# A second state of a Mamba sum kept in a tile of its own, and another queue and pace for the convolution weights, in a four-layer conv/attention kernel

## The chip, the core and the metric

The kernel runs on one core of a Trainium2 chip. The metric is the device time of one execution in microseconds (us). The core has five engines that run side by side and meet at semaphores: TensorE (PE, with its weight loads shown apart as PEld), VectorE (DVE), ScalarE (ACT), GpSimd (POOL) and SyncE (SP), which here only issues DMA transfers. ScalarE can issue transfers too.

## What is computed

Four layers follow each other on an input x of 2 images, 256 channels, 32 x 32 pixels, all in float32: a vision Mamba block pair (layer 0), a convolution that makes a 7 x 7 attention over neighbours (layer 1), a linear attention with a mixture of experts (layer 2), and a softmax attention with a mixture of experts (layer 3). The change lies in layer 0 and in a preparation for layer 1 that is done meanwhile. Of the reference this is what matters:

```python
# layer 0, twice (m1, m2); u has 1024 tokens an image, 512 inner channels d, 16 states n
xs    = silu(causal_conv4(u @ in_w_left))
dt, Bm, Cm = split(xs @ xproj_w)
delta = softplus(dt @ dt_w + dt_b)
dA    = exp(delta[..., None] * A);  dBu = delta[..., None] * Bm * xs[..., None]
h_t   = dA_t * h_(t-1) + dBu_t                 # for each d and n
y_t   = sum over n of h_t[d, n] * C_t[n]       # einsum('bdn,bn->bd')
out   = ((y + xs * D) * silu(u @ in_w_right)) @ out_w + out_b
# layer 1: a dilated 7x7 convolution (w1) followed by a 1x1 convolution (w2) with 49 outputs
```

The two convolutions of layer 1 have nothing between them, so the kernel first multiplies the weights: w1 and w2 give one 7 x 7 convolution with 49 outputs, the "taps".

## The kernel before, in words

**Units.** The 2048 tokens are cut into four chunks of 512, and each of the two Mamba blocks goes over them, which makes eight units, 0 to 7 (line 608). Inside a unit, `scan` (L415) walks over the 16 states n and, for each, over four groups dc of 128 inner channels: 64 slots. For one state:

- GpSimd makes dBu as two tiles `h` of 128 x 1024 each: du times a broadcast row `b` of B (L461). The rows `b` come from DRAM through SyncE's queue (L457).
- ScalarE makes `da` = exp(delta * A) into PSUM, one 128 x 512 tile a slot (L468).
- VectorE runs the recurrence over the 512 tokens, in place on `h` (L472, one scan a slot).
- TensorE turns `h` so that tokens lie on partitions (L440, 16 transposes a state into four PSUM tiles `ht`).
- The turned tile times C_n is summed into `ya` by VectorE (L449, a multiply-add of 128 x 512, four a state). For two states it is done by ScalarE instead (L447, a copy with a scale): state 0 starts `ya`, and state ASIDE = 10 goes into a tile `yb` of its own, so that VectorE has nothing to do for it. The turning and summing of state n run in the four slots of state n + 1, as the generator `rest` (L434).

There are six buffers of `h`, three of `da`, three of `ht`.

**What is woven in.** While a unit scans, `paced` (L552) hands out steps of other generators by slot: the `back` (L485) of the unit before, the `front` (L293) of the unit after, and the taps. The back's first nine steps (GATED) fall in slots 0 to 35, its other seven in slots 40 to 61; the front's first 22 steps (HEAD) in slots 0 to 38, its last 16 in slots 38 to 62. The front's last steps make delta and du for the next unit: 16 tensor operations on GpSimd (L405, L407, L409, L411) fed by ScalarE (L393, L396, L403, L404). The back multiplies the gate, and for each dc it gathers y on TensorE: one matmul with the diagonal of D (L507), then for `ya` and again for `yb` four matmuls with the identity, that turn the sum back and add it in PSUM (L512). VectorE multiplies the result with the gate (L516). Then come the output matmuls (L524, L528), a norm, and the addition to x on GpSimd (L543, and L548 in block m2, which adds the input x loaded by L547).

**The taps** (`Taps.make`, L675). The weights are 7 x 14 blocks of 128 x 128. A part of four blocks (the last of a row has two) is loaded through SyncE's queue (L686), turned on TensorE (L700), copied by ScalarE (L702), multiplied with w2 (L706), copied by ScalarE (L711) and stored to DRAM through SyncE's queue (L714). That makes 28 parts of two steps each and one last step for the bias. Unit 0 takes 12 steps and units 1 to 6 take 9 each, in slots 40 to 63 (L630, L631). In unit 7 the taps' place is taken by the convolution itself, on TensorE (L650, L762), which reads them back.

The Tile framework orders each engine's instructions by a priority that follows the order of emission and by when it expects a buffer, so an engine's order is near the emitted one but not the same.

Of the kernel before, what the change touches and what calls it, by code (L numbers as in the profile page):

```python
# [19 lines left out]
P = 128  # L20
# [213 lines left out]
class Mamba:  # L234

    ASIDE = 10
    GATED = 9
    HEAD = 22  # L240

# [173 lines left out]
    def scan(self, j, before, between, start=False):  # L415
# [6 lines left out]
        xs, bd, ct, delta, du = self.chunks[j]  # L422
        state, first = self.state, self.first(j)
        ya = self.two.tile([P, TPC, DI], F32, tag="ya", name=f"{m}_ya_{j}")
        yb = self.one.tile([P, TPC, DI], F32, tag="yb", name=f"{m}_yb_{j}")
        self.chunks[j] = xs, ya, yb
        G = 2
        half = [P, G, TC]

# [4 lines left out]
        def rest(n, hs):  # L434


            for i in range(TPC):
                ps = self.ps_ht.tile([P, DI], F32, tag="ht", name=f"{m}_ht_{j}_{n}_{i}")
                for dc in range(NDC):
                    nc.tensor.transpose(  # L440
                        ps[:, dc * P : (dc + 1) * P], hs[dc // G][:, dc % G, i * P : (i + 1) * P],
                        net.ident,
                    )
                yield
                c = ct[:, i, n : n + 1]
                if n in (0, self.ASIDE):
                    nc.scalar.activation((yb if n else ya)[:, i, :], ps, AF.Copy, scale=c)  # L447
                else:
                    nc.vector.scalar_tensor_tensor(  # L449
                        ya[:, i, :], ps, c, ya[:, i, :], ALU.mult, ALU.add  # L450
                    )
                if i == 0 and first:
                    keep(n, hs)

        for n in range(NS):
            b = scanp.tile([P, TC], F32, tag="b", name=f"{m}_b_{j}_{n}", bufs=4)
            nc.sync.dma_start(b, bd[n].partition_broadcast(P))  # L457
            hs = []
            for g in range(NDC // G):
                h = scanp.tile(half, F32, tag="h", name=f"{m}_h_{j}_{n}_{g}", bufs=6)  # L460
                (nc.vector if start and n == 0 else nc.gpsimd).tensor_mul(  # L461
                    h, du[:, g * G : (g + 1) * G, :], b.unsqueeze(1).to_broadcast(half)
                )
                hs.append(h)
            for dc in range(NDC):
                da = self.ps_da.tile([P, TC], F32, tag="da", name=f"{m}_da_{j}_{n}_{dc}")
                i = dc * NS + n
                nc.scalar.activation(  # L468
                    da, delta[:, dc, :], AF.Exp, scale=self.aneg[:, i : i + 1]
                )  # L470
                h = hs[dc // G][:, dc % G, :]
                nc.vector.tensor_tensor_scan(  # L472
                    h, da, h, 0.0 if first else state[:, n, dc : dc + 1], ALU.mult, ALU.add
                )
# [10 lines left out]
    def back(self, j):  # L485
# [19 lines left out]
        for dc in range(NDC):  # L505
# [4 lines left out]
            for k, ya in enumerate(sums):  # L510
                for i in range(TPC):
                    nc.tensor.matmul(  # L512
                        ps[:, i * P : (i + 1) * P], lhsT=ya[:, i, dc * P : (dc + 1) * P],
                        rhs=net.ident, start=False, stop=(k == 1 and i == TPC - 1),
                    )
            nc.vector.tensor_mul(y[:, dc, :], ps, gate[:, dc, :])  # L516
            yield
# [18 lines left out]
        yield  # L536
        for cc in range(NCC):
            ps = net.transposed(self.ps_mm, tiles, cc, "mm")
            r = self.one.tile([P, TC], F32, tag="r", name=f"{m}_r_{j}_{cc}", bufs=3)
            nc.scalar.activation(  # L540
                r, ps, AF.Identity, scale=net.col(f"{m}_ln_w", cc), bias=net.col(f"{m}_ln_b", cc)
            )
            nc.gpsimd.tensor_add(xt[:, cc, tok], xt[:, cc, tok], r)  # L543
            if self.x is not None:
                x = self.one.tile([P, TC], F32, tag="r", name=f"{m}_x_{j}_{cc}", bufs=3)
                at = j % (HW // TC) * TC
                nc.sync.dma_start(x, self.x[j // (HW // TC), cc, :, at : at + TC])  # L547
                nc.gpsimd.tensor_add(xt[:, cc, tok], xt[:, cc, tok], x)  # L548
# [26 lines left out]
def layer0(net, x, x_dram, m1, m2, load_image, taps, conv_dram, lg):  # L575
# [5 lines left out]
    with (  # L581
# [32 lines left out]
        for u, (m, j) in enumerate(units):  # L614
# [12 lines left out]
            steps += [(f, 16, 38, 62) for f in fronts] + [(b, 7, 40, 61) for b in done]  # L627
            steps += [(rest, 1, 62, 63)]
            if u + 1 < len(units):
                n = 9 if u else 12  # L630
                steps += [(islice(aside, n), n, 40, 63)]  # L631
            else:
                last.close()
                m.ps_da = last.enter_context(tc.tile_pool(name="m_da2", bufs=2, space=PSUM))
# [28 lines left out]
class Taps:  # L663
# [11 lines left out]
    def make(self, psum, dram):  # L675

        net, nc, pool = self.net, self.net.nc, self.pool
        self.made = [dram.tile([P, 14, NTAP], F32, name=f"taps_{u}") for u in range(7)]
        parts = [(u, k) for u in range(7) for k in range(0, 14, 4)]
        loaded = []  # L680

        def load():
            u, k = parts[len(loaded)]
            n = min(4, 14 - k)
            w = pool.tile([P, 4, P], F32, tag="w1", name=f"w1_{u}_{k}", bufs=3)
            nc.sync.dma_start(  # L686
                w[:, :n, :], self.w1[:, u, k // NCC : (k + n) // NCC].rearrange("p v c o -> p (v c) o")
            )
            loaded.append(w)

# [2 lines left out]
        for i, (u, k) in enumerate(parts):  # L693
            if len(loaded) < len(parts):
                load()
            w = loaded[i]
            n = min(4, 14 - k)
# [1045 lines left out]
```

## Time and profile before

The time before is 2189.04 us, the median of 3 runs (2184.31 to 2190.55). The profiled execution took 2186.6 us.

| | |
|---|---|
| layer 0 | from the start to about 1110 us |
| eight units, from the first scan to the next unit's first | 112.1, 127.0, 126.4, 124.5, 121.1, 124.8, 124.6, and 117.6 us for the last one's scans |
| granted TensorE clock, mean | 0.918 of full speed |

In the profile each engine's busy time is a union of its instructions. A group of instructions is a line of the kernel on one engine; behind the first bar stand the busy time in us and the mean ns of one instruction, behind the second the idle time of the engine just before them and what ended it. A multiply in float32 appears as two matmul passes, so the 128 identity matmuls of `ya` are counted as 256. On VectorE and ScalarE an instruction starts a little before the one ahead of it ends, so the distance of starts is shorter than the duration.

### The profile page before, as it was taken

Reading aid. Unit: us, or ns where it says so; the run is one execution under the profiler, and the core shown is the slowest. Engines: PE = TensorE matmul, PEld = TensorE weight load, DVE = VectorE, ACT = ScalarE, POOL = GpSimd, SP = SyncE. Lnnn points to the kernel's source line nnn. Section 1 sums busy time; section 2 is a strip of 40 time slices with the busy share of each in tenths; the row PEclk is TensorE's granted clock in tenths of the full one; section 3 lists DMA queues with packets and bytes.
Section 4 is the critical chain, followed back from the end, with each engine's and each line's share of the span. In section 5 each row is a group of like instructions: output and inputs, shape, how many; then the busy total and the mean of one; then the engine's idle time right before and its main releaser. Section 6 shows DMA issues by size and latency. Waiting matters only on the chain.

```text
span 2186.6 us, 27311 instructions
## 1 busy us (share of the span) xinstructions
PE 1894.0 (87%) x9652; PEld 1335.5 (61%) x9652; DVE 1400.3 (64%) x2210; ACT 959.2 (44%) x1610; POOL 1028.9 (47%) x726
## 2 busy tenths in 40 slices
PE   6888898898978888788999989949999599859996
PEld 2464555556555655454646556539999467649995
DVE  6999998999999999899005475752222544432223
ACT  4676677767777767645013454411111132301111
POOL 3796787959698686965025420012332000023331
PEclk9869889898989889899999999969999799979997
DMA  2121121111212111310030100028998200059997
GB/s 106 45 68 39 37 69 35 58 35 45 62 47 60 38 49 35 85 42 17 0 64 1 48 15 10 20 82 306 326 329 323 82 10 10 20 206 327 329 323 292
DMA packets 90499, 223.87 MB, mean 102 GB/s; under 512 B 35467, under 2 KB 51728, under 8 KB 79732
## 3 DMA queue, kind: packets, MB, share of 16 engines
q1 hardware_dynamic: 77636, 198.29, 27.1%
q0 software_dynamic: 7728, 19.15, 2.9%
q10 hardware_dynamic: 4992, 4.59, 0.7%
q8 instruction: 81, 1.33, 0.3%
q14 instruction: 62, 0.51, 0.1%
HBM read 204.60 MB, written 19.37 MB: 102 GB/s over the span
## 4 chain that ended last, share of the span: by engine, by line
PE 32%; DVE 22%; issue 19%; POOL 11%; ACT 10%; DMA 5%; POOLq 0%; SPq 0%; DVEq 0%; ACTq 0%
DVE m_h L472 11%; DVE m_ya L449 6%; PE acc L762 3%; POOL x L1520 3%; POOL l_yd L1570 3%; PE m_ht L440 3%; PE early_acc L762 3%; PE av L1276 3%; ACT m_da L468 2%; PE sc L1250 2%; DMA l_yd<-y,target 2%; POOL m_h L461 2%; PE h L1099 2%; PE m_xd_ps L351 1%; PE w L1108 1%
## 5 line engine op out<-in xcount | busy, mean ns | idle before, releaser
L461 POOL TENSOR_TENSOR m_h<-m_du,m_b 128x1024 f32<-128x1024 f32 x254 | 594.5, 2364 | 196.0 <-PE m_ht L440 95.8
L440 PE MATMUL m_ht<-ident,m_h 128*128 128x128 f32 x2048 | 361.2, 305 | 119.4 <-DVE m_ya L449 83.9
L440 PEld LDWEIGHTS m_ht<-ident,m_h 128*128 128x128 f32 x2048 | 259.5, 154 | 317.8 <-DVE m_ya L449 112.7
L468 ACT ACTIVATE m_da<-m_delta,m_aneg 128x512 f32<-128x512 f32 x512 | 349.5, 690 | 220.8 <-DVE m_h L472 220.1
L1520 POOL DMA_INDIRECT x<-l_zd,source x82 | 84.8, 1034 | 573.1 <-DVE source L1465 217.1
L449 DVE SCALAR_TENSOR_TENSOR m_ya<-m_ht,m_ct,m_ya 128x512 f32<-128x512 f32 x448 | 320.2, 733 | 18.4 <-PE m_ht L440 17.5
L472 DVE TENSOR_TENSOR_SCAN m_h<-m_da,m_state,m_h 128x512 f32<-128x512 f32 x256 | 318.7, 1271 | 14.7 <-POOL m_h L461 8.7
L472 DVE TENSOR_TENSOR_SCAN m_h<-m_da,m_h 128x512 f32<-128x512 f32 x256 | 303.3, 1210 | 23.6 <-ACT m_da L468 13.1
L1550 PEld LDWEIGHTS h<-xts,we 128*128 128x128 f32 x2528 | 298.4, 194 | 7.1 <-issue 3.4
L1550 PE MATMUL h<-xts,we 128*128 128x128 f32 x2528 | 299.4, 277 | 2.2 <-issue 1.7
L1557 DVE TENSOR_TENSOR hid<-hid,h 128x512 f32<-128x512 f32 x79 | 54.3, 688 | 258.9 <-PE h L1550 258.9
L1556 ACT ACTIVATE hid<-h 128x512 f32<-128x512 f32 x79 | 47.2, 598 | 384.6 <-issue 324.0
L1564 PE MATMUL o<-we,hid 128*128 128x256 f32 x632 | 150.4, 380 | 2.2 <-DVE y L1569 1.6
L1570 POOL DMA_INDIRECT l_yd<-y,target x79 | 79.3, 1003 | 142.6 <-DVE y L1569 136.3
L1564 PEld LDWEIGHTS o<-we,hid 128*128 128x128 f32 x632 | 113.7, 190 | 15.7 <-DVE y L1569 2.8
L336 PE MATMUL m_conv<-m_pre,m_taps 128*128 128x512 f32 x240 | 114.6, 596 | 6.7 <-ACT m_gate L498 5.6
L762 PE MATMUL early_acc<-x,early 128*98 128x448 f32 (+21 forms) x308 | 97.0, 447 | 0.0
L762 PE MATMUL acc<-x,pair 128*98 128x416 f32 (+21 forms) x308 | 93.6, 452 | 0.0
L1569 DVE COPY y<-o 128x256 f32<-128x256 f32 x79 | 33.6, 425 | 69.6 <-PE o L1564 69.6
L309 PE MATMUL m_in<-x,m_in_sb 128*128 128x512 f32 x128 | 68.8, 663 | 9.8 <-ACT m_pre L313 6.9
L762 PEld LDWEIGHTS acc<-x,pair 128*98 128x98 f32 x308 | 47.7, 167 | 39.9 <-issue 34.5
L528 PE MATMUL m_out<-m_out_sb,m_xs 128*128 128x256 f32 x256 | 68.7, 397 | 0.0
(318 smaller groups left out, 2843.3 us busy)
## 6 DMA issues: line engine op xcount, KB each, us to landing
we<-in_l_experts_dram SPq DMA_DIRECT2D x82, 1536.0 KB
m_b<-m_bd SPq DMA_DIRECT2D x128, 256.0 KB
w<-in_l_w_dram SPq DMA_DIRECT2D x21, 256.0 KB
l_zd<-l_z SPq DMA_DIRECT2D x7, 512.0 KB
l_yl<-l_yd SPq DMA_DIRECT2D x10, 256.0 KB
l_yl<-l_yd ACTq DMA_DIRECT2D x10, 256.0 KB
early<-taps SPq DMA_DIRECT2D x7, 343.0 KB
pair<-taps SPq DMA_DIRECT2D x7, 343.0 KB
```

The source lines that it names most:

```text
L309: nc.tensor.matmul(ps, lhsT=self.in_sb[:, kc, mc * P : (mc + 1) * P], rhs=self.xt[:, kc, tok], start=(kc == 0), stop=(kc == NCC - 1),)
L336: nc.tensor.matmul(ps, lhsT=self.taps[:, dc * 4 + k, :], rhs=pre[:, dc, k : k + TC], start=(k == 0), stop=(k == 3),)
L440: nc.tensor.transpose(ps[:, dc * P : (dc + 1) * P], hs[dc // G][:, dc % G, i * P : (i + 1) * P], net.ident,)
L449: nc.vector.scalar_tensor_tensor(ya[:, i, :], ps, c, ya[:, i, :], ALU.mult, ALU.add)
L461: (nc.vector if start and n == 0 else nc.gpsimd).tensor_mul(h, du[:, g * G : (g + 1) * G, :], b.unsqueeze(1).to_broadcast(half))
L468: nc.scalar.activation(da, delta[:, dc, :], AF.Exp, scale=self.aneg[:, i : i + 1])
L472: nc.vector.tensor_tensor_scan(h, da, h, 0.0 if first else state[:, n, dc : dc + 1], ALU.mult, ALU.add)
L762: nc.tensor.matmul(a[:, lo - 16 * k : hi - 16 * k, co : co + n], lhsT=lhsT, rhs=self.x[:, kc, b, lo - r0 : hi - r0, ci : ci + n], start=(u ...
L1520: nc.gpsimd.indirect_dma_start(out=x, out_offset=None, in_=zd[:, :], in_offset=bass.IndirectOffsetOnAxis(ap=source[:, g : g + 1], axis=0), ...
L1550: nc.tensor.matmul(ps[:, at], lhsT=w12[:, s, kc, at], rhs=xt[:, kc * P : (kc + 1) * P], start=(kc == 0), stop=(kc == NCC - 1),)
L1564: nc.tensor.matmul(ps[:, :C], lhsT=ht[:, mc * P : (mc + 1) * P], rhs=w[:, 8 + mc, :], start=(mc == 0), stop=(mc == NHC - 1),)
L1570: nc.gpsimd.indirect_dma_start(out=yd[g], out_offset=bass.IndirectOffsetOnAxis(ap=target[:, g : g + 1], axis=0), in_=y, in_offset=None, bo ...
```

## The change

A second state, 13, gets a tile of its own; the other one moves from state 10 to state 9. ScalarE fills both, and the back of each unit adds three sums on TensorE instead of two. The new tile takes 8 KB a partition; to make room, the rows `b` have three buffers instead of four, the tag `r` of the back two instead of three, and the parts of the taps have three blocks instead of four. That makes 35 parts of two steps. Units 1 to 6 take 10 steps each, and all steps are spread over slots 24 to 63 instead of 40 to 63. The made taps are stored through ScalarE's queue. The aim is to take work from VectorE and to keep the taps' stores from standing in SyncE's queue in front of the rows `b`.

```diff
-    ASIDE = 10
+    ASIDE = 9, 13
...
-        yb = self.one.tile([P, TPC, DI], F32, tag="yb", name=f"{m}_yb_{j}")
-        self.chunks[j] = xs, ya, yb
+        sums = {0: ya}
+        for n in self.ASIDE:
+            sums[n] = self.one.tile([P, TPC, DI], F32, tag=f"ya{n}", name=f"{m}_ya{n}_{j}")
+        self.chunks[j] = xs, *sums.values()
...
-                if n in (0, self.ASIDE):
-                    nc.scalar.activation((yb if n else ya)[:, i, :], ps, AF.Copy, scale=c)
+                if n in sums:
+                    nc.scalar.activation(sums[n][:, i, :], ps, AF.Copy, scale=c)
...
-            b = scanp.tile([P, TC], F32, tag="b", name=f"{m}_b_{j}_{n}", bufs=4)
+            b = scanp.tile([P, TC], F32, tag="b", name=f"{m}_b_{j}_{n}", bufs=3)
...
-                        rhs=net.ident, start=False, stop=(k == 1 and i == TPC - 1),
+                        rhs=net.ident, start=False, stop=(k == len(sums) - 1 and i == TPC - 1),
...
-            r = self.one.tile([P, TC], F32, tag="r", name=f"{m}_r_{j}_{cc}", bufs=3)
+            r = self.one.tile([P, TC], F32, tag="r", name=f"{m}_r_{j}_{cc}", bufs=2)
...
-                x = self.one.tile([P, TC], F32, tag="r", name=f"{m}_x_{j}_{cc}", bufs=3)
+                x = self.one.tile([P, TC], F32, tag="r", name=f"{m}_x_{j}_{cc}", bufs=2)
...
-                n = 9 if u else 12
-                steps += [(islice(aside, n), n, 40, 63)]
+                n = 10 if u else 12
+                steps += [(islice(aside, n), n, 24, 63)]
...
-        parts = [(u, k) for u in range(7) for k in range(0, 14, 4)]
+        parts = [(u, k) for u in range(7) for k in range(0, 14, 3)]
...
-            n = min(4, 14 - k)
-            w = pool.tile([P, 4, P], F32, tag="w1", name=f"w1_{u}_{k}", bufs=3)
+            n = min(3, 14 - k)
+            w = pool.tile([P, 3, P], F32, tag="w1", name=f"w1_{u}_{k}", bufs=3)
...
-            wt = pool.tile([P, TC], F32, tag="w1t", name=f"w1ts_{u}_{k}", bufs=1)
+            wt = pool.tile([P, 3 * P], F32, tag="w1t", name=f"w1ts_{u}_{k}", bufs=1)
...
-            out = pool.tile([P, 4, NTAP], F32, tag="taps", name=f"taps_sb_{u}_{k}", bufs=3)
+            out = pool.tile([P, 3, NTAP], F32, tag="taps", name=f"taps_sb_{u}_{k}", bufs=3)
...
-            nc.sync.dma_start(self.made[u][:, k : k + n, :], out[:, :n, :])
+            nc.scalar.dma_start(self.made[u][:, k : k + n, :], out[:, :n, :])
```

More of the change, by code (lines that the diff above doesn't have):

```diff
@@ L683, in load @@
             u, k = parts[len(loaded)]
-            n = min(4, 14 - k)
-            w = pool.tile([P, 4, P], F32, tag="w1", name=f"w1_{u}_{k}", bufs=3)
+            n = min(3, 14 - k)
+            w = pool.tile([P, 3, P], F32, tag="w1", name=f"w1_{u}_{k}", bufs=3)
             nc.sync.dma_start(
-                w[:, :n, :], self.w1[:, u, k // NCC : (k + n) // NCC].rearrange("p v c o -> p (v c) o")
+                w[:, :n, :], self.w1[:, u].rearrange("p v c o -> p (v c) o")[:, k : k + n]
             )
@@ L696, in make @@
             w = loaded[i]
-            n = min(4, 14 - k)
+            n = min(3, 14 - k)
             ps = psum.tile([P, TC], F32, tag="mm", name=f"w1t_{u}_{k}")
```

## The prediction

> **What bounds the kernel now.** I began with the page: the busy shares and the groups of the scan.
>
> ```profile
> PE 1894.0 (87%) x9652; PEld 1335.5 (61%) x9652; DVE 1400.3 (64%) x2210; ACT 959.2 (44%) x1610; POOL 1028.9 (47%) x726
> ...
> L461 POOL TENSOR_TENSOR m_h<-m_du,m_b 128x1024 f32<-128x1024 f32 x254 | 594.5, 2364 | 196.0 <-PE m_ht L440 95.8
> L449 DVE SCALAR_TENSOR_TENSOR m_ya<-m_ht,m_ct,m_ya 128x512 f32<-128x512 f32 x448 | 320.2, 733 | 18.4 <-PE m_ht L440 17.5
> L472 DVE TENSOR_TENSOR_SCAN m_h<-m_da,m_state,m_h 128x512 f32<-128x512 f32 x256 | 318.7, 1271 | 14.7 <-POOL m_h L461 8.7
> ```
>
> Taken alone this says VectorE: its scans and multiply-adds hardly ever wait. But GpSimd waits 95.8 us for turned tiles, so I looked at when it does. The timeline of GpSimd in unit 4 shows it: after a wait of 2.75 us for a free buffer, from the product for state 10 on, it never stops until the next unit has begun.
>
> ```profile
> 613.73 11.66 POOL L461 TENSOR_TENSOR m_h<-m_du,m_b 128x1024 f32<-128x1024 f32 x5 [2.75 <-ACT m_delta L389]
> 625.33 1.30 POOL L405 TENSOR_TENSOR m_du<-m_e,m_du 128x512 f32<-128x512 f32 x1
> ...
> 661.98 4.68 POOL L461 TENSOR_TENSOR m_h<-m_du,m_b 128x1024 f32<-128x1024 f32 x2
> ```
>
> The next unit's first scan starts at 664.37, just when the first of the last two products ends. So each unit has two stretches: A, from its first scan to the product for state 10; B, from there to the next unit's first scan. Busy time by stretches, A and B of units 4 and 5, then unit 7 and the tail behind its last scan (columns: window, length, then busy us and count of PE, PEld, DVE, ACT, POOL, then granted clock, DMA share, GB/s):
>
> ```profile
> 543.20:613.70 70.50, 64.64 (x297) 37.44 (x296) 68.59 (x77) 51.56 (x92) 48.97 (x25) 1.00 0.19 56
> 613.70:664.40 50.70, 40.01 (x220) 30.54 (x219) 46.23 (x61) 40.83 (x73) 50.02 (x31) 0.83 0.17 53
> 664.40:738.30 73.90, 67.41 (x288) 39.02 (x288) 70.55 (x75) 49.54 (x71) 46.77 (x22) 0.93 0.19 47
> 738.30:789.10 50.80, 40.65 (x215) 31.34 (x214) 47.06 (x59) 39.38 (x60) 50.16 (x31) 0.80 0.14 38
> 913.80:1031.30 117.50, 101.38 (x500) 60.64 (x498) 115.19 (x134) 61.10 (x89) 81.96 (x39) 0.99 0.16 40
> 1031.30:1110.20 78.90, 78.80 (x337) 47.46 (x337) 11.49 (x38) 9.74 (x13) 7.38 (x13) 1.00 0.05 13
> ```
>
> B lasts 50.7 or 50.8 us in both, and GpSimd is busy for all but 0.7 of it. That is its work: 13 products of 2.33 (states 10 to 15, and the next unit's first) and 16 operations of about 1.25 for the next unit's delta and du make 50.3. VectorE has 3.7 to 4.5 us to spare in B. In A VectorE (97%) and TensorE (92%) are both nearly full. Unit 7 has no front and is VectorE's (98%); the tail is TensorE's (99.9%).
>
> The chain of work that ended last shows where in A TensorE takes over. These are a step of y in unit 4, the second such in unit 5, and one in the tail:
>
> ```profile
> 590.23 1.92 PE m_xd_ps L351 x4
> 592.14 0.26 PE m_ht L440
> 592.40 0.86 PE m_y L507 x2
> 593.26 1.78 PE m_y L512 x16
> 595.05 0.44 PE m_ht L440 x4
> 595.49 1.85 PE m_xd_ps L351 x4
> ...
> 732.04 2.92 PE m_y L512 x16
> ...
> 1052.36 1.78 PE m_y L512 x16
> ```
>
> TensorE's queue is in order, so the y sums stand in front of the matmuls of x_dbl and of transposes that free `h` for GpSimd. Of four y steps, unit 4 has one on the chain (593), unit 5 two (715.65, and 732.04, which ran in a stretch of half clock).
>
> **What the Trainium skill says.** "TensorE: Matmul & The Clock Gate", Part 1 (engine queue depths): ScalarE, VectorE and GpSimd are strict first-in-first-out, and only weight loads go ahead on TensorE. The trace agrees: GpSimd waits 81.5 us in units 1 to 6 for transposes that stand behind other matmuls. The same part: TensorE's clock drops to half after an idle window. The trace has 1.00 in A of unit 4, 0.93 in A of unit 5 and about 0.8 in B, where TensorE has least to do. "ScalarE: Activation LUTs", What ACT_TABLE_LOAD costs: an activation with one pointer operand is 280 ns plus 0.833 ns an element (707 ns for 512), and successive ones overlap by some 93 ns. The copies of L447 take 0.68, and start 0.57 to 0.62 apart. "DMA: Bandwidth & Descriptors", Issuing engines are not separate DMA queues: another issuer saves only the time of the issue. Here one is 0.40 us on SyncE (L714) and 0.31 on ScalarE (L359).
>
> **The change, part by part.**
>
> - VectorE loses four multiply-adds a unit (states 9 and 13 leave, 10 comes back). In VectorE's timeline their starts are 0.65 us apart: 2.6 us a unit. In units 0 to 6 both states' sums fall in slots 40 to 43 and 56 to 59, which is B, where GpSimd sets the end. A scan can start earlier only as far as its product is ready; at the ends of units 1 to 6 the first product of state 15 is there 0 to 0.5 us before its scan. So I count 0.5 us for each of seven units: -3.5. In unit 7 the whole counts: -2.6.
> - ScalarE gets four more copies (0.6 each, 2.4 a unit). Those of state 9 fall on slots 40 to 43, where it is full (exp and ln of the front, two table loads: busy 8.36 of 8.42 us in unit 4) and VectorE waits 1.2 us for `da`. Queued behind them are `da` for the next scans and L403/L404, which GpSimd's L405 needs. L404 ends at 621.7 and L405 starts at 625.33: 3.6 us of slack, against 2.4 for the copies. The later `da` is hidden too: at states 11 and 12 a product is ready 4 to 7 us before its scan. Nothing.
> - TensorE gets a third sum: per step of y eight more passes. Sixteen take 1.78 us, so 0.89, or 1.46 at half clock. In A, on the chain: one step in even units (0.89), two in odd ones (0.89 + 1.46). Three units of each: 2.7 + 7.0 = +9.7. In unit 7's scans one step on the chain, +0.9. In the tail all four steps are on the chain: 4 x 0.89 = +3.6.
> - The taps leave slots 40 to 63 for 24 to 63: steps are 3.9 slots apart, so four of ten (two parts) are now in A, where none was. A part of three is three transposes (0.60 for four, so 0.45) and six passes (0.84 for eight, so 0.63): 2.2 us a unit on TensorE, and on ScalarE two copies (0.45, 0.25) and an issue (0.31), 2.0 a unit. If all lay on the chain, 2.2 a unit or +13; if TensorE's idle time in A (5.9 and 6.5 us) took it, nothing. I take a third: +4. What the end of the units gains (VectorE's waits for `da` behind bunched taps) lies in B behind GpSimd: nothing.
> - The store on ScalarE adds 35 issues of 0.31 us and waits for its own copy; behind it is `da`, mostly ahead of the scan by 0.5 to 3 us. What it frees on SyncE's queue held up nobody: no wait for `b` shows, and in units 1 to 6 a row is issued 16 us or more ahead of its product. Three buffers make that about two products, 9 us in a row at the least, and x of 256 KB landed 3.76 us after its issue. Nothing. With two `r` buffers the second x is loaded only once the first is added. GpSimd has an addition and a product (3.5 us) in between: at most 0.5 us, in two units. Nothing.
>
> Sum: -3.5 - 2.6 + 9.7 + 0.9 + 3.6 + 4 = +12, so 2201 us.
>
> **The rivals.** *VectorE is the bound.* Its 98% in unit 7 and its small idle time speak for it; then 2.6 us is saved in all eight units, -20.8, the tail gives back 3.6, and 2172 comes out. Against it: B is the same 50.7 us in units with different VectorE work. *TensorE's idle time in A takes the sums and the taps.* 5.9 us is there and 3.6 + 2.2 is asked for; left are -3.5 - 2.6 + 0.9 + 3.6, about 2187, no change. Against it: TensorE's idle time is waiting for others, not to be filled at will. *ScalarE delays GpSimd.* If the four copies, a taps copy and an issue all get in front of L404 (2.4 + 0.8 + 0.3) and the `da` queue, L405 waits and B grows 1 to 2 us in units 0 to 6; with the main case's terms that is about 2211.
>
> **How the numbers follow.** Main case 0.45; VectorE bound 0.28; idle time 0.17; ScalarE 0.10. Faster by over 0.3% (below 2182.5): the VectorE case and a little of the next, since extra TensorE work can also keep the clock up in A of odd units: 0.31. Within: 0.18. Slower (above 2195.6): 0.51, the main case less its lower part, and ScalarE's. The range goes from just under the VectorE case, 2170, to all the taps on the chain and some delay by ScalarE, 2216.
>
> **What would show it.** B should stay at 50 to 51 us with GpSimd full, though VectorE's busy time there falls by about 2.6; A should grow, odd units more; the chain should have L512 x24 with 2.7 us a step; the tail should grow by 3.6. I am wrong if B gets shorter (GpSimd's order changed, or it wasn't the bound), if A shrinks (clock, or the taps' new place), or if GpSimd shows waits for ScalarE in B.

## The result and the profile after

The changed kernel takes 2250.97 us, the median of 4 runs (2249.59 to 2252.14); the kernel before, run beside it, takes 2189.6 (2184.31 to 2190.55). The ratio is 1.0285, with a 95% interval of 1.0267 to 1.0303: slower by 62 us. Forecast were 2201, at most 2216. The direction was right, the size was off by 50 us.

All of the loss lies in layer 0. From the trace of each kernel, in us (A and B as in the prediction; the last column is everything behind the tail):

| | A, units 1 to 6 | B, units 1 to 4 | B, units 5 and 6 | unit 0 | scans of unit 7 | tail | rest |
|---|---|---|---|---|---|---|---|
| before | 442.1 | 204.3 | 102.0 | 112.1 | 117.6 | 78.9 | 1076.4 |
| after | 465.2 | 211.9 | 127.7 | 114.0 | 117.1 | 84.0 | 1074.9 |
| difference | +23.1 | +7.6 | +25.7 | +1.9 | -0.5 | +5.1 | -1.5 |

The page of the changed kernel, busy shares and the groups of the scan, to lay beside those of before:

```profile
PE 1927.2 (86%) x9908; PEld 1361.9 (61%) x9908; DVE 1383.0 (62%) x2178; ACT 981.8 (44%) x1656; POOL 1028.6 (46%) x726
...
L463 POOL TENSOR_TENSOR m_h<-m_du,m_b 128x1024 f32<-128x1024 f32 x254 | 594.6, 2365 | 244.1 <-PE m_ht L442 114.5
...
L474 DVE TENSOR_TENSOR_SCAN m_h<-m_da,m_state,m_h 128x512 f32<-128x512 f32 x256 | 317.0, 1266 | 34.8 <-ACT m_da L470 23.6
...
L451 DVE SCALAR_TENSOR_TENSOR m_ya<-m_ht,m_ct,m_ya 128x512 f32<-128x512 f32 x416 | 295.8, 731 | 36.5 <-PE m_ht L442 36.0
```

GpSimd works as much as before (1028.6 against 1028.9) and waits longer. VectorE has its 32 multiply-adds less, 17 us of work, but the idle time before its scans that start from a kept state (the second row) and before its multiply-adds has about doubled (14.7 to 34.8, 18.4 to 36.5). So no single instruction runs slower; the engines wait more for each other.

The stretches show where: A and B of units 4 and 5, and the tail (columns as in the prediction).

```profile
561.50:637.20 75.70, 68.71 (x329) 42.07 (x329) 68.56 (x77) 51.80 (x93) 46.59 (x24) 0.95 0.17 51
637.20:689.90 52.70, 39.53 (x206) 26.85 (x204) 43.60 (x56) 42.00 (x74) 50.60 (x31) 0.90 0.19 53
689.90:767.00 77.10, 69.13 (x330) 42.19 (x330) 70.82 (x77) 50.83 (x75) 46.27 (x22) 0.96 0.16 43
767.00:829.10 62.10, 44.21 (x204) 31.70 (x203) 44.73 (x55) 41.60 (x64) 56.29 (x35) 0.75 0.19 55
...
1088.90:1172.90 84.00, 83.97 (x371) 51.41 (x370) 10.66 (x36) 11.13 (x15) 7.39 (x13) 1.00 0.04 12
```

B of unit 4 has grown by 2.0 us, and GpSimd, which filled it before, now has 2.1 us idle in it. B of unit 5 has grown by 11.3. A of unit 4 has grown by 5.2 and A of unit 5 by 3.2.

The plainest account is VectorE's waits from the first scan of unit 0 to the last of unit 7. Before, and then after:

```profile
DVE m_h L472 <- POOL m_h L461: 19.2, 13, 4.9
DVE m_h L472 <- ACT m_da L468: 19.0, 23, 2.5
DVE m_ya L449 <- PE m_ht L440: 17.5, 26, 2.2
```

```profile
DVE m_h L474 <- ACT m_da L470: 47.2, 22, 10.2
DVE m_ya L451 <- PE m_ht L442: 36.0, 34, 3.3
DVE m_h L474 <- POOL m_h L463: 23.9, 16, 3.6
DVE ln_st L160 <- PE m_out L530: 21.8, 6, 5.3
```

(Columns: us in total, times, longest.) The units last 978.0 us before and 1035.8 after, +57.8. VectorE is busy for 919.4 and 902.9, so 16.5 less: the saving is real. Its idle time goes from 58.6 to 132.9, +74.3, and the rows say for what: ScalarE's `da` +28, turned tiles from TensorE +19, the output matmuls (for the norm's statistics, L160) +22, GpSimd's products +5. The new waits take 4.5 times what the work gave. Of the 47.2 us for `da`, 18.6 are two waits that come from the buffers of `r` (below); without them `da` has grown by 9.6 only.

**What the output matmuls' row hides.** Here is ScalarE in unit 4 of the changed kernel, at state 10:

```profile
639.65 1.91 ACT L393 ACTIVATE m_e<-m_e 128x2048 f32<-128x2048 f32 x1
...
643.04 2.01 ACT L396 ACTIVATE m_ln<-m_e,one 128x2048 f32<-128x2048 f32 x1
...
645.57 0.67 ACT L449 ACTIVATE m_ya<-m_ht,m_ct 128x512 f32<-128x512 f32 x1
...
646.75 0.46 ACT L704 COPY w1ts<-w1t 128x384 f32<-128x384 f32 x1
...
647.82 1.28 ACT L470 ACT_TABLE_LOAD   x1
649.12 0.69 ACT L470 ACTIVATE m_da<-m_delta,m_aneg 128x512 f32<-128x512 f32 x1
```

and VectorE at the same time:

```profile
649.36 0.43 DVE L160 BATCH_NORM_STATS2 ln_st<-m_out 128x6 f32<-128x256 f32 x1 [3.66 <-PE m_out L530]
649.84 1.22 DVE L474 TENSOR_TENSOR_SCAN m_h<-m_da,m_h 128x512 f32<-128x512 f32 x1
```

Two copies of state 9 (at 645.57 and 647.11) and one of the taps stand between the front's `ln` and the table load behind which `da` waits, so the first `da` runs from 649.12 to 649.81. In VectorE's queue a statistic of the norm stands ahead of the next scan; the matmuls it needs end at 649.3 on TensorE, which is busy 10.3 of the 11.8 us of this state. So the row gives the 3.66 us to the output matmuls, but the scan starts at 649.84, 0.03 us after its `da`: without the statistic it would have waited as long. In the six places where this wait shows, five scans start 0.02 to 0.04 us after their `da` has ended; only in unit 6 was `da` ready before. In these five ScalarE is what was waited for, and the wait for the output matmuls lies in its shadow. The state takes 11.75 us where it took 8.42; over units 1 to 6 it takes 12.1 where it took 8.4, 22 us in all.

The copies of state 9 explain less than half of this. The same instructions of ScalarE before, where the state begins at 616.48 (after: 639.62):

```profile
615.12 1.91 ACT L393 ACTIVATE m_e<-m_e 128x2048 f32<-128x2048 f32 x1
...
618.35 2.01 ACT L396 ACTIVATE m_ln<-m_e,one 128x2048 f32<-128x2048 f32 x1
...
621.74 1.28 ACT L468 ACT_TABLE_LOAD   x1
```

From the end of `ln` to the table load it is 2.77 us instead of 1.39, where the copies stand; and the front's `exp` (L393) begins 0.03 us after the state's first scan instead of 1.36 before it. As means of units 1 to 6, `da` resumes 3.35 us later in the state, of which 2.0 are the later `exp` and 1.5 the longer stretch up to the load (`exp` and `ln` themselves lie 0.1 closer). The runs below tell the two apart: with the copies of states 9 and 13 alone `exp` is not late and the stretch is 1.2 us longer; with the taps alone `exp` is 2.4 us late and the stretch 0.5 longer. Where `exp` is late, ScalarE waits longer for the matmuls that feed the instructions ahead of it (L385): 27.3 us in the units after, 18.1 with the taps alone, 6.6 before, 2.1 with the copies alone.

**Why B of units 5 and 6 is long.** The end of unit 5 on ScalarE, GpSimd and VectorE:

```profile
821.61 0.78 ACT L542 ACTIVATE m_r<-mm_t,cols_sb 128x512 f32<-128x512 f32 x1 [8.86 <-POOL x L545]
...
811.09 9.26 POOL L463 TENSOR_TENSOR m_h<-m_du,m_b 128x1024 f32<-128x1024 f32 x4
820.30 1.27 POOL L545 TENSOR_TENSOR x<-x,m_r 128x512 f32<-128x512 f32 x1
...
823.07 1.28 DVE L474 TENSOR_TENSOR_SCAN m_h<-m_da,m_state,m_h 128x512 f32<-128x512 f32 x1 [8.40 <-ACT m_da L470]
```

With two buffers of `r`, and the loaded x taking one of them, the second half of `r` waits until GpSimd has added the first. GpSimd has four products ahead of that addition, not one. `da` stands behind the waiting `r`, and VectorE stands for 8.4 us (10.2 in unit 6).

### The profile page after: what moved, and what is told of

Its sections match the earlier page's. It is cut to its first block, busy times and chain, and to the rows that moved or that the text cites. A ratio compares the mean times of both kernels' runs of the same rounds, so it can differ in the third digit from the quotient of the medians.

```text
span 2247.7 us, 27840 instructions
## 1 busy us (share of the span) xinstructions
PE 1927.2 (86%) x9908; PEld 1361.9 (61%) x9908; DVE 1383.0 (62%) x2178; ACT 981.8 (44%) x1656; POOL 1028.6 (46%) x726
## 4 chain that ended last, share of the span: by engine, by line
PE 28%; issue 18%; DVE 16%; POOL 13%; ACT 5%; DMA 4%; POOLq 0%; ACTq 0%; DVEq 0%
DVE m_h L474 8%; DVE m_ya L451 4%; POOL x L1522 3%; PE acc L764 3%; POOL m_h L463 3%; POOL l_yd L1572 3%; PE av L1278 2%; PE sc L1252 2%; PE early_acc L764 2%; DMA l_yd<-y,target 2%; PE h L1101 2%; PE m_ht L442 2%; PE w L1110 1%; PE m_y L514 1%; PE m_out L530 1%
## 5 line engine op out<-in xcount | busy, mean ns | idle before, releaser
L442 PE MATMUL m_ht<-ident,m_h 128*128 128x128 f32 x2048 | 365.5, 306 | 110.5 <-DVE m_ya L451 74.3
L474 DVE TENSOR_TENSOR_SCAN m_h<-m_da,m_state,m_h 128x512 f32<-128x512 f32 x256 | 317.0, 1266 | 34.8 <-ACT m_da L470 23.6
L451 DVE SCALAR_TENSOR_TENSOR m_ya<-m_ht,m_ct,m_ya 128x512 f32<-128x512 f32 x416 | 295.8, 731 | 36.5 <-PE m_ht L442 36.0
L1558 ACT ACTIVATE hid<-h 128x512 f32<-128x512 f32 x79 | 47.2, 597 | 384.2 <-issue 319.0
L514 PEld LDWEIGHTS m_y<-ident,m_ya 128*128 128x128 f32 x768 | 94.3, 197 | 16.7 <-issue 16.7
L514 PE MATMUL m_y<-ident,m_ya 128*128 128x128 f32 x768 | 94.4, 279 | 0.0
L496 PE MATMUL m_g<-x,m_gate_sb 128*128 128x512 f32 x128 | 67.5, 631 | 19.7 <-ACT m_r L542 18.4
```

The source lines that it names most:

```text
L442: nc.tensor.transpose(ps[:, dc * P : (dc + 1) * P], hs[dc // G][:, dc % G, i * P : (i + 1) * P], net.ident,)
L451: nc.vector.scalar_tensor_tensor(ya[:, i, :], ps, c, ya[:, i, :], ALU.mult, ALU.add)
L474: nc.vector.tensor_tensor_scan(h, da, h, 0.0 if first else state[:, n, dc : dc + 1], ALU.mult, ALU.add)
L514: nc.tensor.matmul(ps[:, i * P : (i + 1) * P], lhsT=ya[:, i, dc * P : (dc + 1) * P], rhs=net.ident, start=False, stop=(k == len(sums) - 1 ...
```

## The experiments

Each time is the median; each ratio is to the kernel before on the same chip, with its 95% interval. The us in the text are the ratio times the kernel before. Three theories stand against each other: the prediction's (GpSimd bounds B, TensorE's sums and taps cost in A, the copies are hidden), ScalarE (the copies and taps delay `da`), and `r` (the buffers).

### The buffers of `r` alone

```diff
-            r = self.one.tile(..., tag="r", ..., bufs=3)
+            r = self.one.tile(..., tag="r", ..., bufs=2)
...
-                x = self.one.tile(..., tag="r", ..., bufs=3)
+                x = self.one.tile(..., tag="r", ..., bufs=2)
```

> The kernel before, with the tag r on two buffers instead of three and nothing else. Theory R (the third user of the tag, the second half's r, must wait for GpSimd's addition of the first half's r, ScalarE stands in order behind it, and so do da and the scans; this happens where the input x shares the tag, at the ends of units 5 and 6): about 22 us slower, 2212 us, all of it in the second stretch (B) of units 5 and 6, where ScalarE shows waits of 8 to 12 us for the addition. Rival (two buffers suffice, as the prediction said, and the long ends of units 5 and 6 come from the taps or the sums): within 1 us of before, 2190 us.

2197.05 us, ratio 1.0049 (1.0033 to 1.0066), +11. B of units 5 and 6 grew by 16.6 us together, A of units 1 to 6 gave 6.1 back and B of units 1 to 4 took 2.6, and ScalarE waits for GpSimd's addition 15.4 us at the longest, where no such wait shows before. The prediction's "nothing" for this edit was wrong.

### The changed kernel with three buffers of `r`, with and without the second state

```diff
-            r = self.one.tile(..., tag="r", ..., bufs=2)
+            r = self.one.tile(..., tag="r", ..., bufs=3)
...
-            w = pool.tile([P, 3, P], F32, tag="w1", ..., bufs=3)
+            w = pool.tile([P, 3, P], F32, tag="w1", ..., bufs=2)
...
-            out = pool.tile([P, 3, NTAP], F32, tag="taps", ..., bufs=3)
+            out = pool.tile([P, 3, NTAP], F32, tag="taps", ..., bufs=2)
```

(the loaded x has three too; the memory comes from the taps' buffers). The second of the two has three buffers of `r` and x as well, leaves the taps' buffers as they are in the changed kernel, and takes one state aside:

```diff
-    ASIDE = 9, 13
+    ASIDE = 10,
```

> The changed kernel with the tag r back on three buffers; the 2 KB are paid by the taps' blocks (two buffers of w1 instead of three, two of the made taps instead of three). Theory R: units 5 and 6 fall to the length of units 3 and 4, about 23 us less, 2228 us. Rival: units 5 and 6 stay long, 2250 us.

> The changed kernel with a single state (10) aside as before and r on three buffers: what stays of the change is the taps (parts of three, 10 steps over slots 24 to 63, stores by ScalarE) and three buffers of b. Theory T (the taps' steps in the first stretch take TensorE and the PSUM banks away from the transposes and from the output matmuls): 12 to 20 us slower than before, 2202 to 2210 us, with first stretches 2 us longer. Theory S (the third sum on TensorE and the copies on ScalarE are what costs): within 4 us of before.

2241.87 us, 1.0262 (1.0245 to 1.0280), +57; and 2202.16, 1.0080 (1.0056 to 1.0105), +17. The first shows that `r` is worth only some 5 us in the changed kernel (B of units 5 and 6 falls by 19.0, but A grows by 4.5, B of units 1 to 4 by 2.8 and unit 7 by 3.8; the smaller weight buffers may have a part in that). The difference of the two, +40, points at the second state, though the two differ in the taps' buffers as well. (The expectations below that speak of smaller weight buffers in both are mistaken: only the first has them.) So I took the parts one by one on the kernel before.

### Does GpSimd bound B?

```diff
         for dc in range(NDC):
+            eng = nc.vector if alone or dc == NDC - 1 else nc.gpsimd
             w = du[:, dc, :]
```

> The kernel before, with the last of the four groups of operations that make delta and du (L405, L407, L409, L411 of dc = 3) on VectorE instead of GpSimd: 5.0 us less a unit for GpSimd in the second stretch, 2.7 us more for VectorE. Theory P (GpSimd bounds the second stretch): units 0 to 6 get 2 to 4 us shorter each, 2162 to 2175 us. Rival V (VectorE bounds): 2.7 us longer in seven units, 2208 us.

2193.83 us, 1.0039 (1.0024 to 1.0053), +8.5. Four of GpSimd's sixteen front operations went to VectorE. Units 1 to 6 gave 11.4 us in A and took 14.5 in B. Neither theory said so. Taking work from GpSimd did not shorten B, as a bound by GpSimd alone would have it. It isn't a clean test, though: the work went to VectorE, and B's first mark moves with GpSimd's own order.

### The second state alone, and its two halves

States 9 and 13 aside in the kernel before, taps and buffers untouched. Both copies go to the one tile that is there; in the first kernel it is summed twice:

```diff
-    ASIDE = 10
+    ASIDE = 9, 13
...
-                if n in (0, self.ASIDE):
+                if n in (0, *self.ASIDE):
...
         y, *sums = self.chunks.pop(j)
+        sums.append(sums[-1])
...
-                        rhs=net.ident, start=False, stop=(k == 1 and i == TPC - 1),
+                        rhs=net.ident, start=False, stop=(k == 2 and i == TPC - 1),
```

The second leaves out the last two of these edits (copies without a third sum), the third has only these two (a third sum without copies).

> The kernel before with the second state aside alone: states 9 and 13 are copied by ScalarE in place of state 10, and TensorE makes three sums; taps, stores, `b` and `r` as before. (Both copies go to one tile, which is summed twice, so that no other buffer has to shrink: state 13's part is counted twice and state 9's is lost; the work is that of the changed kernel.) The prediction's terms (-3.5 -2.6 +9.7 +0.9 +3.6) give +8, 2193. The difference of two earlier runs, changed kernel with three `r` buffers with and without the second state, gives about +40, 2225, if the smaller weight buffers of those two runs had no part in it. VectorE as the bound: 2168.

> The same without the third sum: only ScalarE's eight copies in place of four, and VectorE's four multiply-adds fewer (state 9's part is lost). The prediction: 2185 - 6 = 2179, since the copies cost nothing. If ScalarE's full slots at state 10 are what costs (the column of state 10 was 3.7 us longer in the changed kernel, in each of six units, and that of state 14 about 1.5): +20 to +30, 2205 to 2215, and the column of state 10 has 12 us again. If VectorE were the bound: 2164.

> The kernel before with a third sum alone: state 10's tile is added twice in each step of y (its part counts twice), 64 more passes of TensorE a unit; nothing else changes. The prediction's term is 9.7 + 0.9 + 3.6 = +14, 2199, with stretch A longer by 0.9 in even and 2.35 in odd units and the tail by 3.6. If TensorE's idle time takes it: +4.5, 2189. If TensorE's order in A is what costs most of the difference of +40: +25 or more, 2210.

2245.53 us, 1.0283 (1.0265 to 1.0301), +62; 2222.75, 1.0184 (1.0166 to 1.0202), +40; 2203.22, 1.0090 (1.0072 to 1.0108), +20. The two halves add up to the whole, and the second state alone costs as much as the whole change. The copies, which the prediction put at nothing (and VectorE's saving at -6), are two thirds of it.

The sum without copies costs 8.5 us in A of units 1 to 6, 3.7 in their B and 6.7 in the tail; unit 7's scans take 0.9 more. One of the four steps on the chain of the changed kernel's tail, all of one length:

```profile
1111.46 2.68 PE m_y L514 x24
```

It is 0.90 longer than before, four times 0.90 in all, as forecast, and the kernel with the sum alone has the same four. Most of the other 3 us of the tail are gate matmuls of the last back: behind the last scan the chain has 14 passes of them with the third sum, and 8 before. In the units the loss fell on even ones (+2.5, +5.4, +4.7 in units 2, 4 and 6; -1.2, +1.4, -0.6 in 1, 3 and 5), not on odd ones.

### Which copies?

```diff
-    ASIDE = 10
+    ASIDE = 10, 13
```

(both copies to one tile, two sums, as with 9, 13); then 9 alone; then 11, 12.

> State 10 stays aside and state 13's copies are added (ASIDE = 10, 13; one tile for both, two sums, so state 10's part is lost): VectorE has four multiply-adds a unit fewer, ScalarE four copies more, in slots 56 to 59. The prediction's terms give 2184 - 6 = 2178. If the copies of state 13, in the column of state 14 where ScalarE has norm, m_r and bunched taps too, carry most of the +39 that states 9 and 13 cost together: +25, 2209, with the columns of states 14 and 15 at 12 us in units 1 to 4.

> State 9 aside in place of state 10, one state as before: the four copies move from slots 44 to 47 to slots 40 to 43, where ScalarE is full (8.4 of 8.4 us). The prediction's view, that four more copies in these slots are hidden: 0, 2184. ScalarE's full slots: the column of state 10 goes from 8.4 to 10 us, that of state 11 loses up to 1; +7 to +12, 2191 to 2196.

> Two states aside where ScalarE has time: states 11 and 12 (ASIDE = 11, 12; one tile, two sums, so state 11's part is lost). Their copies fall in the columns of states 12 and 13, where ScalarE is busy 3.7 of 6.0 and 5.2 of 8.1 us and VectorE is full. The number of copies, multiply-adds and sums is that of the kernel with states 9 and 13, which took +39. If it is the place of the copies that costs: 2178 to 2184, no change or a little faster. If it is their number (ScalarE's work): +30, 2214. If VectorE's work were what counts: 2164.

2222.69 us, 1.0171 (1.0135 to 1.0207), +37; 2193.18, 1.0034 (1.0021 to 1.0048), +7; 2212.05, 1.0133 (1.0093 to 1.0173), +29. State 13 costs most: with 10 and 13 aside, states 14 and 15 of units 1 to 6 take 38.5 us more and the other states together no more than before. But the place isn't all: where ScalarE has time, at states 11 and 12, two states still cost +29. No wait for stores or weights shows in that kernel's trace (its fastest run, 2204), and still VectorE waits 53 us for `da`. So full slots, the theory I had, explain a part only; a second state cost in all three places tried.

With states 10 and 13 aside, the end of unit 2 shows what a late unit meets. SyncE's queue, ScalarE and VectorE:

```profile
402.41 28.33 SPq L457 DMA_DIRECT2D m_b<-m_bd  x4
430.79 0.42 SPq L714 DMA_DIRECT2D taps<-taps_sb  x1
...
414.02 0.24 ACT L711 COPY taps_sb<-taps_ps 128x98 f32<-128x98 f32 x1 [0.28 <-PE taps_ps L706]
...
434.25 0.32 ACT L711 COPY taps_sb<-taps_ps 128x196 f32<-128x196 f32 x1 [9.48 <-DMA taps<-taps_sb]
...
435.20 1.22 DVE L472 TENSOR_TENSOR_SCAN m_h<-m_da,m_h 128x512 f32<-128x512 f32 x1 [8.85 <-ACT m_da L468]
```

From 402.41 to 430.74 SyncE issues four rows `b`, each only when a product of GpSimd has freed its buffer, and stands in between. The taps' stores are behind them: the first, of a copy that ended at 414.26, is issued at 430.79, 16.5 us later. ScalarE's fourth taps copy needs the buffer that this store reads, and waits 9.48 us; `da` is behind the copy, and VectorE waits 8.85.

Rows that wait for buffers are not new: SyncE waits for GpSimd 810 us in all in the kernel before. What is new is the order of its queue. Before, at the end of unit 4 (unit 2 has the same order):

```profile
647.14 11.28 SPq L457 DMA_DIRECT2D m_b<-m_bd  x2
658.48 0.42 SPq L714 DMA_DIRECT2D taps<-taps_sb  x1
658.99 0.38 SPq L686 DMA_DIRECT2D w<-in_l_w_dram  x1
666.68 0.32 SPq L457 DMA_DIRECT2D m_b<-m_bd  x1
```

There the first store and load of weights come ahead of the last row. With 10 and 13 aside this row is ahead of all of them. With states 9 and 13, TensorE stood in the same way for a load of weights behind rows `b`:

```profile
563.91 0.66 PE L700 MATMUL w1t<-ident,w 128*128 128x128 f32 x2 [8.90 <-DMA w<-in_l_w_dram]
```

In the kernel before these two waits come to 0.8 and 1.8 us in all.

### The copies by themselves

```diff
-                if n in (0, self.ASIDE):
+                if n in (0, self.ASIDE, 13):
                     nc.scalar.activation(...)
-                else:
+                if n not in (0, self.ASIDE):
                     nc.vector.scalar_tensor_tensor(...)
```

> The kernel before with state 13's copies added on ScalarE, and VectorE's multiply-adds of state 13 kept (the copies go to state 10's tile, whose part is lost). ScalarE's copies in slots 56 to 59 by themselves: if they are what cost +37 with states 10 and 13 aside: 2220 or more. If it was the new order of the queues that came with fewer multiply-adds on VectorE: 2185 to 2195.

2204.63 us, 1.0087 (1.0063 to 1.0110), +19, between the two answers, and not a clean price of the copies either: VectorE's multiply-adds of state 13 wait 20.1 us in all for ScalarE's copies of the same tiles, a wait that only this kernel has. What it does show is that four more copies alone don't delay `da`: VectorE waits 15.4 us for it in the units, less than before, and no wait for a store or for weights is there. With VectorE's multiply-adds of state 13 taken away as well (states 10 and 13 aside), which should help, it is 18 us slower, `da` is waited for 56.5 us, stores 18.2 and weights 15.6. GpSimd's order in unit 2 is the same in both, but SyncE's isn't: with the copies alone, the first store and load still come ahead of the last row (416.17 and 416.64 against 424.38). So the only edit between the two kernels, fewer multiply-adds on VectorE, also put that row ahead of the stores. What the copies cost by their own time and what by such a new order stays open, as no run holds the order fixed; the stops at SyncE can't be all of it, since states 11 and 12 cost +29 without any.

### The weights loaded on the other queue

The kernel with the copies of states 9 and 13 and no third sum, and:

```diff
-            nc.sync.dma_start(
+            nc.scalar.dma_start(
                 w[:, :n, :], self.w1[...])
```

> The kernel of states 9 and 13 without the third sum (2222), with the taps' weights loaded through ScalarE's queue instead of SyncE's, so that they no longer stand behind the rows `b` of the next unit. In that kernel TensorE waited 8.9 and 7.9 us for such a load. If these waits are on the path: 2222 - 16 = 2206. If ScalarE and TensorE waiting for each other is enough to make the delay (units 2 and 4 are as long and show no such wait): 2215 to 2222.

2215.92 us, 1.0134 (1.0107 to 1.0162): 7 us (by the medians) to 11 us (by the ratios) below the kernel that it changes. TensorE's waits for weights (16.8 us) are gone, but only a part of them shows in the time: at state 14 VectorE now waits 4.0 us at a stretch for a turned tile in unit 2 and 7.0 us for `da` in unit 3. A part of the wait that was taken away was taken up by others.

### The taps' change, whole, in part and with the copies

The whole (parts of three, from slot 24, stored by ScalarE) in the kernel before; the spread alone:

```diff
-                steps += [(islice(aside, n), n, 40, 63)]
+                steps += [(islice(aside, n), n, 24, 63)]
```

and the whole together with the copies of states 9 and 13, without the third sum.

> The kernel before with the change of the taps alone (parts of three, ten steps from slot 24 on, stores on ScalarE's queue), its buffers of `b`, `r` and weights as many as before. The prediction's term: +4, 2189. The earlier run of the changed kernel without the second state, with three `r` buffers and fewer weight buffers, gave +17; if its smaller buffers had no part in it, 2202 here; if they had, between.

> The taps in parts of four and stored by SyncE as before, their nine steps a unit spread over slots 24 to 63 instead of 40 to 63. The whole taps change alone took +21. If it is the taps' TensorE and ScalarE work in the stretch that TensorE fills (the prediction's cause, +4 there): +15 to +20, 2200 to 2205. If it is the store on ScalarE's queue: 0 to +4 here, 2186.

> States 9 and 13 copied aside without the third sum (+39 alone), together with the whole change of the taps (+21 alone), buffers of `b` and `r` as before. If the two add up: 2184 + 60 = 2244. If they act on the same waits, that is, if in units 1 to 4 the end of the unit stands because TensorE and ScalarE wait for each other and for the taps' weights, and the spread of the taps removes that (B of units 1 to 4 was 59 to 61 with the second state alone and is 53 in the changed kernel): 2244 - 32 = 2212.

2204.29 us, 1.0100 (1.0068 to 1.0132), +22; 2195.84, 1.0044 (1.0027 to 1.0062), +10; and 2225.20, 1.0179 (1.0155 to 1.0204), +39. Alone the taps cost +22, of which the spread makes about half: nine of its ten are in A. On top of the copies they cost nothing (+39 with, +40 without). The stops behind SyncE's rows are gone, and VectorE's waits for `da` in the units go from 56.6 to 31.4 us; but A is 20 us longer than with the copies alone, and at state 10 VectorE waits for the output matmuls:

```profile
DVE m_h L472 <- ACT m_da L468: 31.4, 20, 4.2
DVE ln_st L160 <- PE m_out L528: 24.3, 6, 5.4
```

where it was 8.3 us with the copies alone, and nothing before. (Four of these six waits end with `da` as well, two do not.) So the change of the taps does what it is for, and pays for it in other slots.

### No state aside

State 10 is added on VectorE too; then the freed memory goes into `h`; then, in the kernel before, unit 7 alone without a state aside.

```diff
-    ASIDE = 10
+    ASIDE = ()
```

```diff
-                h = scanp.tile(half, F32, tag="h", ..., bufs=6)
+                h = scanp.tile(half, F32, tag="h", ..., bufs=8)
```

```diff
+        last = self.x is not None and j == NCH - 1
+        aside = -1 if last else self.ASIDE
+        sums = {0: ya}
+        if not last:
+            sums[aside] = self.one.tile([P, TPC, DI], F32, tag="yb", ...)
```

> No state aside but state 0: state 10 is added by VectorE as well, four copies a unit leave ScalarE, 64 passes a unit leave TensorE, and VectorE has four multiply-adds more, in stretch B. By the runs, which gave +20 for a third sum and +37 for four more copies, a gain: 2150 to 2170. By the prediction's terms turned round (sums -14, VectorE +6): 2177. If VectorE is the bound: 2184 + 21 - 4 = 2201.

> No state aside but state 0 (2186), and the 8 KB that this frees spent on two more buffers of `h` (eight instead of six). If GpSimd bounds stretch B, as the prediction said: it waits some 20 us a unit in A for free buffers, two more let it run one state (two products of 2.33) ahead, and B is shorter by up to 4.7 us in units 0 to 6: down to 2153. If VectorE, now with four multiply-adds more, and the waits of the queues for each other set it: 2175 to 2187.

> The kernel before, with no state aside in unit 7 alone: units 0 to 6 keep theirs. In the kernel with none aside, unit 7's scans took 117.9 us (117.5 before) and the tail behind them 74.1 (78.9 before), so -4.4, 2180. If VectorE's four multiply-adds more are paid in full in unit 7: +2.6 - 4.8, 2182.

2186.53 us, 1.0023 (1.0010 to 1.0035); 2183.66, 0.9984 (0.9971 to 0.9997); 2184.62, 0.9995 (0.9983 to 1.0006). The windows of unit 3, A and B, with no state aside:

```profile
419.30:487.60 68.30, 62.67 (x266) 34.50 (x265) 66.72 (x74) 48.74 (x73) 44.37 (x21) 0.98 0.18 52
487.60:545.80 58.20, 43.02 (x209) 31.92 (x208) 52.51 (x65) 38.49 (x58) 54.16 (x33) 0.74 0.18 52
```

A is 5.4 us shorter than before and B 7.4 longer, and in B neither GpSimd (54.2) nor VectorE (52.5 of 58.2) is full. Over units 1 to 6 A gives 40 us and B takes 41.7. With eight buffers of `h`, A gives 61.5 and B takes 53.6: GpSimd does run ahead, and most of the time comes back later in the unit. Against the kernel with none aside and six buffers, the six units are 9.6 us shorter, 1.6 a unit, where up to 4.7 were expected of a bound by GpSimd. In unit 7 alone, the scans take 2.1 us more and the tail 4.8 less, which the time hardly shows. None of these is a version worth having: the best, none aside with eight `h`, gains 3.5 us on the kernel before, under 0.2%, with an interval that nearly reaches 1.

## Why the prediction was right and wrong

**Right: slower, and by which kinds of things.** The third sum costs in A and in the tail, with L512 (now L514) x24 and 2.68 us a step; the four steps of the tail cost the +3.6 that was forecast. VectorE's work fell by 16.5 us in the units and nothing came of it. A grew in all of units 1 to 6, though more in even ones (5.8, 5.2, 3.6) than in odd ones (2.5, 2.7, 3.2), against the forecast. The direction came out right on a part of the loss: the sum and the taps were to cost +18, less 6 that VectorE saves, while the largest part stood at nothing.

**Wrong, the largest: "ScalarE gets four more copies ... Nothing."** This is the step that failed. Measured +40 for states 9 and 13 and +37 for 10 and 13, VectorE's saving included. The step saw that `da` stands behind the copies, in the strict order that the Trainium skill states for ScalarE ("TensorE: Matmul & The Clock Gate", Part 1, engine queue depths); the runs agree with that order: `da` stood behind one taps copy, and VectorE 8.85 us behind `da`. Two things in it were wrong. It took `da` for hidden because products were ready 4 to 7 us before their scans at states 11 and 12; but a scan needs both, so an early product gives a late `da` no room. And it looked at the slots of state 9 alone. State 9 in place of 10 costs +7; the four copies that are really added are state 13's, in slots 56 to 59, and with them states 14 and 15 take 38.5 us more. VectorE waits 19.0 us for `da` before, 56.6 with the copies of 9 and 13 alone and 47.2 in the changed kernel (18.6 of these behind `r`). How the copies make `da` late is shown only in part: the four copies with the multiply-adds kept leave the wait at 15.4, and taking those multiply-adds away changed SyncE's order as well.

**Wrong: "B ... where GpSimd sets the end."** B was 50.7 us with GpSimd full, which I took for a bound. B of units 1 to 4 is 59 to 61 with the copies alone and GpSimd's busy time in it grows too, to 58 to 59: it has by then begun four products of the next unit instead of two, before that unit's first scan. So GpSimd is nearly full between these marks in both kernels, and what counts as B's work isn't fixed. Fewer operations on GpSimd (and more on VectorE) did not shorten the units (1.0039); more room ahead of it gave 1.6 us a unit, a third of what a bound would have allowed. GpSimd has a part in the unit's length, but doesn't set it alone.

**Wrong: "With two `r` buffers ... Nothing."** +11 alone. The step counted one addition and one product of GpSimd between the two halves (3.5 us); in unit 5 there were four products in front of the first addition (9.26 us) and a load of x after it. The wait was named, its length wasn't read from GpSimd's queue, where before the additions came late as well.

**Wrong in size: the taps, +4.** Alone +22, about half from the spread. **And the store on ScalarE's queue, "What it frees on SyncE's queue held up nobody":** true of the kernel before (0.8 us), false with states 9 and 13 aside (9.6 us for stores and 16.8 for loads in the kernel without the third sum), though not with 11 and 12. The Trainium skill says that another issuer saves only the time of an issue ("DMA: Bandwidth & Descriptors", Issuing engines are not separate DMA queues). Here the place in the queue matters more: on SyncE, with states 10 and 13 aside, a store stood 16.5 us behind rows that waited for buffers, against 0.42 us for the issue itself.

**Wrong in size: the sum in the units,** +13 against +10.6, and in even units rather than odd; its tail is 6.7 against 3.6, mostly by the gate's matmuls. In the changed kernel the tail has grown by 5.1.

**Rivals.** VectorE as the bound fails: its work fell and the units grew. TensorE's idle time taking the sum fails: +20. "ScalarE delays GpSimd", the one with the least chance, had the right engine, but not the path: GpSimd's L405 waits for ScalarE only once, 2.3 us, in the changed kernel, and the longer waits are VectorE's for `da`.

**The parts and the whole.** Alone they are +62 (second state), +22 (taps) and +11 (`r`), 95 us; together +62. Of the 33 us between, some 22 are the taps, which cost nothing on top of the copies: the stops at SyncE's rows, which come with the copies, are gone with them. `r` costs 5 instead of 11 in the changed kernel, as far as the run with smaller weight buffers tells. The last 5 I can't assign. Three buffers of `b` weren't tried alone; the run with them, the taps and three `r` (+17) isn't slower than the taps alone (+22).

## What to carry to other kernels

An edit that adds small work to an in-order engine is priced by what stands behind it in that queue and who waits for that, at every place where it adds work, not by the engine's share of busy time or by one slack: four copies on a ScalarE that is busy 44%, in place of four multiply-adds of VectorE, cost 37 to 40 us here. Where a framework orders the queues, look whether the edit has moved other instructions too. A stretch in which one engine is full is shown to be bound by it only when taking work from that engine, without giving it to another full one, shortens it. Costs of parts that act on the same waits don't add up: measure the parts alone and in pairs before giving any of them a number.

## What was not expected of the hardware

A store stood 16.5 us in SyncE's queue behind rows that waited for buffers, and held up ScalarE and VectorE by 9.48 and 8.85 us through a buffer of 196 numbers a partition. Nothing else was new: the durations of single instructions are the same in both kernels (2.36 us a product, 0.69 `da`, 0.73 a multiply-add), and so is the mean granted clock of the two traces, 0.918.
